# Attention scores as three float32r products, with engine queues ordered by a list schedule

## The chip, the cores and the metric

The kernel runs on one NeuronCore of a Trainium2 chip. The metric is the device time of one execution in microseconds (us); the time before is 1512.19 us, the median of 3 runs (1509.23 to 1512.96). Engines are named as in the profile: PE is the matrix engine (its weight loads, PEld, overlap its matmuls), DVE the vector engine, ACT the scalar engine, POOL the GpSimd engine; SP issues the DMAs. [...] Each engine takes its instructions in the order in which they stand in its queue, and waits at an instruction whose inputs are not ready.

## The reference

One transformer block in fp32: attention with 16 heads of 128 on 2 batches of 1024 tokens and a model width of 512, then a gated feed-forward layer with ternary weights and 1365 hidden columns, each between layer norms and with a residual.

```python
q = jnp.einsum('bsd,hed->bhse', x, W_Q)
k = jnp.einsum('bsd,hed->bhse', x, W_K)
v = jnp.einsum('bsd,hed->bhse', x, W_V)
scores = jnp.einsum('bhse,bhme->bhsm', q, k) * scale
scores = jnp.where(causal, jnp.float32(-1000000000.0), scores)
pattern = jax.nn.softmax(scores, axis=-1)
z = jnp.einsum('bhsm,bhme->bhse', pattern, v)
out = jnp.einsum('bhse,hde->bsd', z, W_O)
...
x = x + _layernorm(_L0_attn_ref(_layernorm(x), W_Q, W_K, W_V, W_O))
x = x + _layernorm(_L0_ffn_ref(_layernorm(x), w1, w3, w2))
```

## The kernel before

Two number formats matter. float32r is a format of PE for 4-byte values that keeps fewer bits of the mantissa. Where the kernel needs an fp32 result from it, it splits an operand into forms: a leading part ("a"), a low part ("l") and a last one ("d", a difference of the two), each exact in float32r. Two products are summed in one PSUM tile `main`, the third goes into a second tile `diff`, and `main` x 4097 - `diff` is the fp32 product (`combine`, lines 453 to 460). Projections of Q, K and V (lines 471, 478, 499) and the output projection (519) are computed so. The scores (line 556) and the products of the softmax weights with V (line 650) are plain fp32 matmuls.

The work goes over 32 heads (n = 0 to 31, 16 for each batch). A head has eight score rows `i` of 128 queries; row i has L = (i + 1) x 128 columns, because of the causal mask. `scores` makes one row: one or two matmuls of at most 512 columns into `s_ps` (two buffers of two PSUM banks each), the mask on the last 128 columns (DVE, line 561), the negated maximum (DVE, 565), the exponential with its sum (ACT, 572), the reciprocal (DVE, 577) and the scaling (ACT, 578) in the SBUF tile `p_sb`, of which there is one for even rows and one for odd. `turn` transposes the row in blocks of 32 into `blocks` (DVE, 604); for each pair of rows a DMA carries them to DRAM (`hop`) and `bring` fetches them back in another order (`pt`, four DMAs), and `values` multiplies them with V and splits the result into forms for the output projection (ACT 662, DVE 667, POOL 670). One pair of heads shares the weights of V and of the output; weights are loaded and split in `load_raw`, `lead_and_low` (ACT 439, POOL 440) and `difference_form` (DVE 446).

The order of the queues is written out by hand. The main loop goes over the score rows of all heads; in each step it does some projections, value products and output products for PE (`fill`, `product`), the scores three rows ahead (`AHEAD`), the transpose of the row two ahead, and one-off work (`side`: weight statistics, ternary weights, the layer norms of the middle, the transposes of the second batch). `behind` and `past` hold an instruction back until a named earlier one stands in its queue, by `tc.issue_after`. The feed-forward stage (from about 1270 us on) runs four blocks of 512 tokens, each with 11 tiles of hidden columns (lines 318 and 933).

## Time and profile before

| | |
|---|---|
| Median of 3 runs | 1512.19 us |
| Span of the profiled execution | 1509.5 us |
| Granted PE clock, mean | 0.997 of full speed |
| Busy of the span: PE, DVE, ACT, POOL | 98%, 72%, 53%, 27% |
| Score matmuls, L556 | 768 records, 289.7 us |
| Mask, L561, and maximum, L565 | 256 each, 75.4 and 193.7 us |
| Exponential, L572, and scaling, L578 | 256 each, 190.0 and 197.7 us |
| Transpose in blocks of 32, L604 | 256, 197.1 us |
| DMA to DRAM and back for the largest pair of rows | 1024 KB in 4.5 us, four of 256 KB in 6.2 us (median, issue to landing) |

The profile is one execution, taken by the hardware profiler. A group line gives the source line, the engine, the operation, the tiles (written <- read), the shape and the count, then after the bar the busy time in us and the mean duration of one in ns, and then the idle time of the engine before it with what ended it. An fp32 matmul of the program is recorded as two MATMUL records. [...] A line of waits reads: who waited, for whom, us in total, how often, and the longest. A line of the timeline begins with the start and the length in us. In a table of stretches, the columns are the length, and for each engine the busy us.

### The profile page before, as it was taken

How to read it: one execution, taken by the hardware profiler on the slowest of the kernel's cores; microseconds unless marked ns; L12 is line 12 of the kernel's file. 1: busy time of each engine (PE TensorE's matmuls, PEld its weight loads, DVE VectorE, ACT ScalarE, POOL GpSimd, SP SyncE). 2: the span in 40 equal slices, each digit the busy share in tenths (PEclk: the TensorE clock that was granted, in tenths of full speed). 3: DMA queues.
4: the chain of work that ended last, by engine and by line, in shares of the span. 5: the costliest groups of instructions: out<-in, count | busy, mean ns of one | idle time of the engine just before them, and what ended most of it. 6: DMA issues, size and time to landing. Idle time of an engine off the chain costs nothing.

```text
span 1509.5 us, 21335 instructions
## 1 busy us (share of the span) xinstructions
PE 1475.6 (98%) x7061; PEld 1184.9 (78%) x7061; DVE 1080.6 (72%) x2123; ACT 792.7 (53%) x1566; POOL 404.3 (27%) x472
## 2 busy tenths in 40 slices
PE   8999999999999999999999999999999999999997
PEld 6778888887878787777778787878787877888885
DVE  7767686878786878787777777777777776664444
ACT  4656555555555555666664555555555464444332
POOL 3222222222223333434433333333322110210010
PEclk9999999999999999999999999999999999999999
DMA  3666767676666675758866666666665677530200
GB/s 123 194 194 186 195 184 200 185 202 184 201 191 172 181 206 183 205 166 249 238 200 190 195 192 196 195 195 189 179 179 166 181 216 228 176 102 19 91 28 29
DMA packets 179894, 263.57 MB, mean 175 GB/s; under 512 B 19188, under 2 KB 120564, under 8 KB 175688
## 3 DMA queue, kind: packets, MB, share of 16 engines
q1 hardware_dynamic: 179784, 262.20, 59.5%
q8 instruction: 57, 0.93, 0.3%
q14 instruction: 53, 0.43, 0.1%
HBM read 160.43 MB, written 101.71 MB: 174 GB/s over the span
## 4 chain that ended last, share of the span: by engine, by line
PE 66%; issue 10%; DVE 9%; DMA 7%; ACT 5%; POOL 2%; SPq 1%; DVEq 0%; POOLq 0%; ACTq 0%
PE mm L650 11%; PE mm L471 10%; PE mm L318 10%; PE s_ps L556 10%; PE mm L499 8%; PE mm L519 6%; PE yp L933 5%; PE mm L478 5%; DVE nm L565 3%; DMA hop<-blocks 2%; ACT p_sb L572 2%; DMA wqk<-wk 2%; ACT p_sb L578 1%; POOL kl L440 1%; DVE blocks L604 1%
## 5 line engine op out<-in xcount | busy, mean ns | idle before, releaser
L572 ACT ACTIVATE p_sb<-s_ps,nm 128x128 f32<-128x128 f32 (+7 forms) x256 | 190.0, 742 | 367.3 <-DVE nm L565 360.8
L556 PE MATMUL s_ps<-k,q 128*128 128x512 f32 (+3 forms) x768 | 289.7, 486 | 0.7 <-ACT p_sb L572 0.7
L650 PE MATMUL mm<-pt,v_sb 128*128 128x256 f32 (+1 forms) x1280 | 271.7, 359 | 11.3 <-ACT q L454 3.7
L650 PEld LDWEIGHTS mm<-pt,v_sb 128*128 128x128 f32 x1280 | 238.1, 190 | 48.8 <-ACT q L454 6.2
L578 ACT ACTIVATE p_sb<-p_sb,ri 128x128 f32<-128x128 f32 (+7 forms) x256 | 197.7, 773 | 33.0 <-DVE ri L577 30.5
L565 DVE TENSOR_REDUCE nm<-s_ps 128x1 f32<-128x128 f32 (+7 forms) x256 | 193.7, 757 | 7.1
L604 DVE STREAM_TRANSPOSE blocks<-p_sb 128x128 f32<-128x128 f32 (+7 forms) x256 | 197.1, 770 | 1.2 <-ACT p_sb L578 0.9
L556 PEld LDWEIGHTS s_ps<-k,q 128*128 128x128 f32 x768 | 132.3, 190 | 69.4 <-issue 61.4
L670 POOL TENSOR_TENSOR zd<-za,zl 128x256 fp32r<-128x256 f32 x128 | 94.7, 739 | 328.0 <-DVE zl L667 319.7
L561 DVE TENSOR_TENSOR s_ps<-s_ps,causal 128x128 f32<-128x128 f32 x256 | 75.4, 295 | 136.1 <-PE s_ps L556 135.6
L499 PE MATMUL mm<-va,xb 128*128 128x256 f32 x512 | 158.5, 310 | 0.0
L499 PE MATMUL mm<-vd,xb 128*128 128x256 f32 x512 | 144.9, 283 | 0.9 <-POOL xb L409 0.9
L499 PE MATMUL mm<-vl,xb 128*128 128x256 f32 x512 | 144.6, 282 | 0.0
L471 PE MATMUL mm<-xb,qa 128*128 128x512 f32 x256 | 119.6, 467 | 1.0 <-ACT xb L407 1.0
L471 PE MATMUL mm<-xb,ka 128*128 128x512 f32 x256 | 112.3, 439 | 0.0
L499 PEld LDWEIGHTS mm<-vl,xb 128*128 128x128 f32 x512 | 97.7, 191 | 7.1 <-issue 4.1
L499 PEld LDWEIGHTS mm<-va,xb 128*128 128x128 f32 x512 | 97.7, 191 | 7.1 <-issue 3.9
L471 PE MATMUL mm<-xb,ql 128*128 128x512 f32 x256 | 101.7, 397 | 0.0
L471 PE MATMUL mm<-xb,kl 128*128 128x512 f32 x256 | 100.7, 393 | 0.1
L499 PEld LDWEIGHTS mm<-vd,xb 128*128 128x128 f32 x512 | 97.7, 191 | 1.1 <-POOL xb L409 1.1
L601 POOL MEMSET blocks<- 128x128 f32 x128 | 26.2, 205 | 263.1 <-DMA hop<-blocks 185.2
L533 DVE TENSOR_TENSOR acc<-acc,mm 128x512 f32<-128x512 f32 x128 | 86.1, 683 | 12.7 <-ACT acc L528 5.4
(162 smaller groups left out, 2777.3 us busy)
## 6 DMA issues: line engine op xcount, KB each, us to landing
hop<-blocks SPq DMA_DIRECT2D x32, 1024.0 KB, 4.5
pt<-hop SPq DMA_DIRECT2D x128, 256.0 KB, 6.2
hop<-blocks SPq DMA_DIRECT2D x32, 768.0 KB, 3.3
pt<-hop SPq DMA_DIRECT2D x128, 192.0 KB, 3.8
hop<-blocks SPq DMA_DIRECT2D x32, 512.0 KB, 3.2
pt<-hop SPq DMA_DIRECT2D x128, 128.0 KB, 3.2
wqk<-wq SPq DMA_DIRECT2D x32, 256.0 KB, 5.2
wqk<-wk SPq DMA_DIRECT2D x32, 256.0 KB, 6.6
```

The lines of the kernel that those rows point to most:

```text
L318: newest[0] = nc.tensor.matmul(ps[:fl, :], lhsT=t[:, c, :], rhs=bl[k][:, c, :], start=(c == 0 and k == 0), stop=(c == NC - 1 and k == 1),)
L471: newest[0] = nc.tensor.matmul(main, lhsT=forms[f][0][:, c, :], rhs=forms[f][1][:, c, :], start=(c == 0 and f == 0), stop=(c == NC - 1 and ...
L499: newest[0] = nc.tensor.matmul((main, main, diff)[f][:, ts(t, 2 * P)], lhsT=forms[f][0][:, c, token], rhs=forms[f][1][:, c, :], start=(t = ...
L519: newest[0] = nc.tensor.matmul((main, main, diff)[f], lhsT=zs[g, t // QT, j][f][:, ts(t % QT, P)], rhs=weights[3, g][f][:, 2 * j : 2 * j + ...
L533: nc.vector.tensor_tensor(dst, dst, diff, ALU.subtract)
L556: newest[0] = nc.tensor.matmul(s_ps[:, ds(k0, kl)], lhsT=proj[n, 0, i // QT][:, ts(i % QT, P)], rhs=proj[n, 1, k0 // TB][:, :kl], start=Tr ...
L565: top = nc.vector.tensor_reduce(nm, s_ps[:, :L], axis=AX.X, op=ALU.max, negate=True)
L572: e = nc.scalar.activation(p_sb[:, :L], s_ps[:, :L], AF.Exp, bias=nm, accum_out=rs)
L578: nc.scalar.mul(p_sb[:, :L], p_sb[:, :L], ri)
L604: turned = nc.vector.transpose(b[:, :, 0 : i + 1, il, :].rearrange("p to t r -> p t to r"), p_sb[:, :L].rearrange("p (b r) -> p b r", r=32),)
L650: newest[0] = nc.tensor.matmul(dst, lhsT=proj[g, 2][:, kt, ts(j, P)], rhs=rhs, start=(kt == 0), stop=(kt == 2 * m + 1),)
L670: nc.gpsimd.tensor_tensor(diff, lead, low, ALU.subtract)
```

## The change

- Q and K are kept in three float32r forms (tiles `q0a`, `q0l`, `q0d` and so on) instead of one fp32 tile. After `combine`, ACT makes the leading form; for Q, DVE makes the low and POOL the last one, for K, POOL the low and DVE the last.
- Each score matmul becomes three float32r matmuls, two into `sm` and one into `sd` (one PSUM bank and two buffers each, in place of the two buffers of `s_ps`). ACT copies `sm`, scaled by -4097, into `p_sb`; DVE applies the mask there (signs are turned, so a maximum), and one DVE instruction per piece of 512 columns adds `sd` and takes the minimum. The exponential reads `p_sb`.
- `issue_after` and the holds of `behind`, `past` and `busy` are gone. All pools are made through `Order`, which knows the tiles, and at the end `arrange` finds the dependences, gives each instruction a cost, runs a list schedule forwards and backwards ten times, keeps the shortest, and fixes each engine's order (SP's DMAs too) by it.
- The transposes of the first batch use `sm` and `sd` buffers; the DMA scratch of the program is set to 512 bytes.

```diff
@@ query_key_unit
-            proj[n, kind, k] = qkpool.tile(
-                [P, TB], FP, name=f"{'qk'[kind]}{k}", bufs=2 if kind == 1 and k == 0 else 1
+            bufs = 2 if kind == 1 and k == 0 else 1
+            raw, lead, low, last = (
+                qkpool.tile([P, TB], dt, name=f"{'qk'[kind]}{k}{f}", bufs=bufs)
+                for f, dt in (("d", FP), ("a", FR), ("l", FR), ("d", FR))
             )
...
-                combine(
-                    proj[n, kind, k], main, diff, SCALE if kind == 0 else 1.0
-                )
+                combine(raw, main, diff, SCALE if kind == 0 else 1.0)
+                if kind == 0:
+                    nc.scalar.mul(lead, raw, LEAD / T12)
+                    nc.vector.scalar_tensor_tensor(
+                        low, lead, -T12, raw, ALU.mult, ALU.add
+                    )
+                    nc.gpsimd.tensor_tensor(last, lead, low, ALU.subtract)
+                else:
+                    nc.scalar.mul(lead, raw, LEAD)
+                    nc.gpsimd.tensor_tensor(low, raw, lead, ALU.subtract)
+                    nc.vector.scalar_tensor_tensor(
+                        last, low, -T12, lead, ALU.mult, ALU.add
+                    )
+                proj[n, kind, k] = lead, low, last
@@ behind (past and busy likewise)
-            with ExitStack() as order:
-                for name in names:
-                    k = len(marks[name]) - 1
-                    k = k if of is None else min(of, k)
-                    order.enter_context(tc.issue_after(marks[name][k]))
-                yield
+            yield
@@ scores
-            s_ps = ps_s.tile([P, S], FP, name="s_ps")
-            for k0 in range(0, L, TB):
-                kl = min(TB, L - k0)
-                newest[0] = nc.tensor.matmul(
-                    s_ps[:, ds(k0, kl)], lhsT=proj[n, 0, i // QT][:, ts(i % QT, P)],
-                    rhs=proj[n, 1, k0 // TB][:, :kl],
-                    start=True, stop=True,
-                )
-            nc.vector.tensor_tensor(
-                s_ps[:, ts(i, P)], s_ps[:, ts(i, P)], causal, ALU.min
-            )
-            nm = small.tile([P, 1], FP, name="nm")
-            top = nc.vector.tensor_reduce(
-                nm, s_ps[:, :L], axis=AX.X, op=ALU.max, negate=True
-            )
+            q = [w[:, ts(i % QT, P)] for w in proj[n, 0, i // QT]]
+            chunks = [(k0, min(TB, L - k0)) for k0 in range(0, L, TB)]
+            diffs = []
+            for k0, kl in chunks:
+                main = ps_s.tile([P, TB], FP, name="sm")[:, :kl]
+                diff = ps_s.tile([P, TB], FP, name="sd")[:, :kl]
+                diffs.append(diff)
+                for f, dst in enumerate((main, main, diff)):
+                    newest[0] = nc.tensor.matmul(
+                        dst, lhsT=q[f], rhs=proj[n, 1, k0 // TB][f][:, :kl],
+                        start=f != 1, stop=f > 0,
+                    )
+                nc.scalar.mul(p_sb[:, ds(k0, kl)], main, -(T12 + 1.0))
+            nm = KEPT
+            for (k0, kl), diff in zip(chunks, diffs):
+                if k0 + kl == L:
+                    nc.vector.tensor_tensor(
+                        p_sb[:, ts(i, P)], p_sb[:, ts(i, P)], causal, ALU.max
+                    )
+                least = small.tile([P, 1], FP, name="nm", bufs=6)
+                top = nc.vector.tensor_tensor_reduce(
+                    p_sb[:, ds(k0, kl)], p_sb[:, ds(k0, kl)], diff, 1.0, nm,
+                    ALU.add, ALU.min, accum_out=least,
+                )
+                nm = least
             rs = small.tile([P, 1], FP, name="rs")
             e = nc.scalar.activation(
-                p_sb[:, :L], s_ps[:, :L], AF.Exp, bias=nm, accum_out=rs
+                p_sb[:, :L], p_sb[:, :L], AF.Exp, bias=nm, scale=-1.0, accum_out=rs
             )
@@ class Order, arrange, at its end
+        order = self.lists(ops, engine, preds)
+        for chain in order.values():
+            for j, k in zip(chain, chain[1:]):
+                self.tc.add_manual_dep(
+                    ops[k], ops[j].name,
+                    mybir.DependencyInfo(
+                        mybir.DependencyClass.NoSync, mybir.DependencyReason.DATA
+                    ),
+                    reason="order",
+                )
@@ class Order, lists
+        rank, best = list(range(n)), None
+        for _ in range(PASSES):
+            start, took, order = work.forward(rank)
+            end = max(map(sum, zip(start, took)))
+            if best is None or end < best[0]:
+                best = end, start, took, order
+            rank = work.backward(start, took)
@@ class Work, forward
+        for _ in range(n):
+            t, e, k = self.next(wait, here, free)
+            order[e].append(k)
+            busy, took = self.costs[k]
+            if self.table[k] not in (0, table):
+                table, busy, took = self.table[k], busy + 1290, took + 1290
+            if e == "SP":
+                wire = max(wire, t) + self.size[k] / 260
+                took = max(1900 + self.size[k] / 260, wire - t + 1500)
+            start[k], tooks[k], free[e] = t, took, t + busy
+            for j in self.follows[k]:
+                ready[j] = max(ready[j], t + self.lag(k, j, took))
+                missing[j] -= 1
+                if not missing[j]:
+                    ripe(j)
@@ the end of the kernel
+    pools.arrange()
@@ kernel
-    nc = bacc.Bacc("TRN2", target_bir_lowering=False, num_devices=1)
+    nc = bacc.Bacc(
+        "TRN2", target_bir_lowering=False, num_devices=1, dynamic_dma_scratch_size=512
+    )
```

`forward` takes, on each engine, the ready instruction of the lowest rank; `backward` computes from the end how late each instruction may start, and that is the next rank.

## The prediction

> **What bounds the kernel now.** I read the page's shares first, then PE's own waits, then the starts of single matmuls in the timeline.

> ```profile
> PE 1475.6 (98%) x7061; PEld 1184.9 (78%) x7061; DVE 1080.6 (72%) x2123; ACT 792.7 (53%) x1566; POOL 404.3 (27%) x472
> ...
> PE mm L650 <- ACT q L454: 3.7, 6, 0.9
> PE mm L650 <- DVE acc L530: 3.2, 2, 1.7
> ...
> 704.31 0.39 PE L471 MATMUL mm<-xb,kl 128*128 128x512 f32 x1
> 704.54 0.39 PE L471 MATMUL mm<-xb,ka 128*128 128x512 f32 x1
> ...
> 179.78 0.28 PE L499 MATMUL mm<-vl,xb 128*128 128x256 f32 x1
> 179.90 0.28 PE L499 MATMUL mm<-vd,xb 128*128 128x256 f32 x1
> ...
> 702.17 0.19 PEld L556 LDWEIGHTS s_ps<-k,q 128*128 128x128 f32 x1 [0.24 <-issue]
> 702.60 0.19 PEld L556 LDWEIGHTS s_ps<-k,q 128*128 128x128 f32 x1 [0.24 <-issue]
> ```

> PE is hardly ever named as waiting (a few us in total). Its busy share overstates, because matmul records overlap; the price of a matmul is the distance to the next start. A float32r matmul of 512 columns costs 0.227 us, one of 256 columns 0.120. An fp32 matmul is recorded as two passes of 0.430 each at 512 columns (0.323 at 384, 0.216 at 256, 0.109 at 128: median starts on L556 and L650), so four times as much per column. Counts times price: 3,360 float32r matmuls of 512 columns (L471, L478, L519, L318, L933) 762.7; 1,536 of 256 (L499) 184.3; value products on L650, 1,024 x 0.216 + 256 x 0.109 = 249.1; scores on L556, per head 4 x 0.109 + 4 x 0.216 + 4 x 0.323 + 12 x 0.430 = 7.75, times 32 = 248.1; 111 transposes 12.1. Sum 1456. The span of 1509.5 is this, plus 1.5 before the first matmul, 9.9 after the last, and 41.7 of waits and slow clock, 12 of them in the first 50 us. So PE's instruction stream sets the time, and about 30 us of waits lie in its middle.

> The other engines, over the ten stretches of 100 us from 150 to 1150 (sum and mean), and the start of the same output products one pair of heads apart in the chain:

> ```profile
> sum 1000.00, PE 987.86 PEld 791.64 DVE 759.16 ACT 550.11 POOL 309.08; mean PE 98.79 PEld 79.16 DVE 75.92 ACT 55.01 POOL 30.91
> ...
> 107.32 4.12 PE mm L519 x18
> 183.21 4.12 PE mm L519 x18
> ```

> A head takes 75.9 / 2 = 37.9 us, of which DVE is busy 28.8, ACT 20.8, POOL 11.7.

> **The change, part by part.** *Scores.* Each fp32 matmul becomes three float32r ones: per head 18 of 512 columns (4.09), 6 of 384 (0.174 on the line through the two measured points: 1.04), 6 of 256 (0.72) and 6 of 128. No row shows float32r at 128 columns: the line gives 0.066, the transposes with 128 columns show 0.109, two fp32 passes 0.218. I take 0.109, the row with this size and a 4-byte operand: 0.65. Sum 6.50 a head, 208.1 in all, a saving of 39.9 us (48 with 0.066, 19 with 0.218). [...] Nothing covers this term: it is PE time.

> *New work on ACT, per head.* 12 copies of the main product out of PSUM, 4,608 columns: rows of 590 ns at 512 and 378 at 256 give 166 + 0.83 a column, 5.8 us; four leading forms at 0.62 (L439), 2.5; exp from SBUF, +0.03 x 8. 20.8 + 8.5 = 29.3.

> *DVE.* The 8 maxima go (6.05 by L565's 193.7 / 32). 12 fused add-and-minimum instructions come, each with a second instruction that reads the accumulator. Nearest for the first is the maximum by form, 290 at 128 and 689 at 512: 157 + 1.04 a column; for the second the one-column L577, 150. 12 x 0.307 + 4.8 = 8.5, net +2.4 (+0.6 without the second instruction; +7.2 if the fused one makes two passes). Four low and last forms at 0.684 (L458): +2.7. The mask of 128 columns moves from PSUM to SBUF at the same 0.295. Together +5.1: 33.9.

> ```profile
> L565 DVE TENSOR_REDUCE nm<-s_ps 128x1 f32<-128x512 f32 x32 | 22.0, 689 | 0.6
> L565 DVE TENSOR_REDUCE nm<-s_ps 128x1 f32<-128x128 f32 x32 | 9.3, 290 | 1.1
> L458 DVE SCALAR_TENSOR_TENSOR q<-mm,q 128x512 f32<-128x512 f32 x64 | 43.8, 684 | 7.8 <-ACT q L454 6.6 <-PE mm L478 1.2
> ...
> 15.29 3.42 POOL L440 TENSOR_TENSOR vl<-wvo,va 128x512 fp32r<-128x512 f32 x2
> 15.80 1.77 DVE L446 SCALAR_TENSOR_TENSOR qd<-ql,qa 128x512 fp32r<-128x512 f32 x1
> ```

> *POOL* gets four subtractions a head at 1.29 (L440): 11.7 + 5.2 = 16.9. The last two rows show what that may cost: a DVE instruction with two SBUF inputs took 1.77 instead of 0.67 while POOL ran. [...] Over the whole run L446 lost little (738 on average against a median of 674), so I add 0.5 a head for the new ones (8 masks, 4 forms); if each lost 1.1 us it would be 13.

> A head then needs PE 37.9 - 1.25 = 36.7, DVE 34.4, ACT 29.3, POOL 16.9: PE stays the longest.

> *The added wait.* The score row now sits in its p_sb tile from the first copy to the DVE transpose, and there is one tile for even rows, one for odd. So the copy of row i+2 waits on ACT for the transpose of row i; behind it on ACT stand the exp of row i+1 and the evacuations that free PSUM for PE. Rows of 1,024, 768, 512 and 256 columns need, end to end (copies, mask, fused pass, exp 0.19 over its scaling row, reciprocal 0.15, scaling by L578, transpose by L604), 7.0 + 5.9 + 4.2 + 3.0 = 20.1 us plus some 28 hand-overs of 0.1. That is 22.9 of 36.7, so each row may queue 3.4 us for free.

> *The queues.* The hand-written order (issue_after) goes; a list schedule fixes each engine's order. On PE it places the first value product a median of 20 to 23 us of PE work behind the score rows that it needs, against 20 to 24 before, so the DMA round trip keeps its cover. SP issues the same 1,010 DMAs, at new places; POOL's new forms stand in one queue with the clearing of blocks, which waited 185 us for DMAs before, and a form stuck there would hold up the next head's scores. Of the 30 us of waits, about 12 are eight single waits of 1 to 2 us beside one-off work (588 to 755 and 1251 us). A schedule that counts that work may save half of them (6); it may also lose as much: -6, bounds -12 and +12.

> Sum on the profiled execution: 1509.5 - 39.9 - 6 = 1463.6. The median of the runs shown is 2.7 above it: 1466.

> **The rivals.**
> *The schedule closes the middle too* (all of those waits, and float32r at 0.066): 1512 - 48 - 25 = 1439, as far as 1452. For it: single matmuls now fill gaps. Against: ACT and DVE are fuller, and the startup and the tail remain.
> *The p_sb pair becomes tight.* DVE at 94% of a head means that a row queues at each of its three DVE steps. At 0.2 us over the free 3.4, four rows and 32 heads add 26: 1492; with 0.3, 1504. Against: in the present trace the long waits of a row are only those before the transpose, which is put off by the hand-written order.
> *The slower one: DVE takes over.* It decides from 9.1 us of added DVE work a head (28.8 + 9.1 = 37.9). A two-pass fused instruction (+7.2) and the forms (+2.7) make 38.7, so 0.8 x 32 = 26 us slower: 1538. For it: no row shows the fused instruction, and POOL contention grows. Against: the rows by form put it at 5.1 to 5.6.
> *The change doesn't do what it says:* float32r at 128 columns for two fp32 passes leaves 19 of the 39.9: 1487. It is in the range.

> **How the numbers follow.** Forecast 1466, 55%, its own range 1453 to 1480. Closing the middle 14%. The p_sb pair, with the dear 128 columns, 17%, one in ten of it ending near no change. DVE 14%, of which 3 is no change and 11 slower. This kernel's measurement tells 0.3%, 4.5 us, from nothing. Faster 0.55 + 0.14 + 0.15 = 0.84; same 0.05; slower 0.11. The range runs from 1443, into the second case, to 1502, through most of the third.

> **What would show it.** Right: float32r score matmuls 0.227 apart at 512 columns, PE named for few waits, the same output products some 73.4 apart per pair of heads, DVE near 90 per 100 us. Wrong: a fused instruction over 0.9 us at 512 columns; ACT's copies waiting for the transpose and PE for that copy; POOL forms waiting behind the clearing; 128-column starts over 0.11.

## The result, and the profile after

The changed kernel takes 1527.67 us (median of 4 runs, 1524.69 to 1533.79) beside 1512.38 us for the kernel before: a ratio of 1.011, 95% interval [1.0087, 1.0132]. The forecast was 1466 us, range 1443 to 1502: wrong in sign.

The engines' row and the chain's shares, from the page of the changed kernel:

```profile
PE 1464.0 (96%) x7445; PEld 1242.0 (81%) x7445; DVE 1267.1 (83%) x2763; ACT 1011.9 (66%) x2078; POOL 590.5 (39%) x600
...
PE 64%; DVE 20%; issue 6%; ACT 4%; DMA 4%; SPq 1%; POOL 1%; DVEq 0%; POOLq 0%; ACTq 0%
```

The chain's shares before:

```profile
PE 66%; issue 10%; DVE 9%; DMA 7%; ACT 5%; POOL 2%; SPq 1%; DVEq 0%; POOLq 0%; ACTq 0%
```

DVE's share of the chain that ended last went from 9% to 20%. PE's named waits add up to 51.5 us; before, they add up to 23.7 (the prediction says "a few us in total"). The longest of them after (who waited, for whom, us in total, times, longest):

```profile
PE sd L875 <- DVE nm L887: 13.0, 19, 2.1
PE sd L875 <- DVE k0d L799: 7.6, 11, 2.0
PE mm L837 <- DVE acc L848: 4.7, 4, 1.6
PE tr L708 <- DVE acc L427: 4.5, 2, 4.1
```

All four are waits for DVE. In the first, the third score product finds both `sd` banks still held by fused passes that DVE has not reached; in the second, the key's last form is late.

The same sum as in the prediction (count times distance between starts) splits the span. The float32r score matmuls are priced at 0.227 apart at 512 columns, 0.176 at 384, 0.120 at 256 and 0.112 at 128. Their medians in this run, with the starts that waited among them, are 0.229, 0.180, 0.120 and 0.1145, which would be 2.4 us more in all; 0.112 is the median of e15, told below, where PE waits least. Rows of the timeline after (start, length):

```profile
870.01 0.40 PE L875 MATMUL sm<-k0a,q1a 128*128 128x512 f32 x1
870.25 0.40 PE L875 MATMUL sm<-k0l,q1l 128*128 128x512 f32 x1
870.48 0.39 PE L875 MATMUL sd<-k0d,q1d 128*128 128x512 f32 x1
870.71 0.22 PE L875 MATMUL sm<-k1a,q1a 128*128 128x128 f32 x1
870.77 0.27 PE L875 MATMUL sm<-k1l,q1l 128*128 128x128 f32 x1
871.68 0.33 PE L875 MATMUL sd<-k1d,q1d 128*128 128x128 f32 x1 [0.64 <-DVE nm L887]
...
312.25 0.22 PE L875 MATMUL sm<-k1a,q1a 128*128 128x128 f32 x1
312.31 0.27 PE L875 MATMUL sm<-k1l,q1l 128*128 128x128 f32 x1
312.42 0.28 PE L875 MATMUL sd<-k1d,q1d 128*128 128x128 f32 x1
312.53 0.65 PE L972 MATMUL mm<-pt,v_sb 128*128 128x256 f32 x2
```

At 312.25 nothing is waited for: behind the first 128-column product the next one starts after 0.06, behind the second and the third after 0.11. Only 43 of the 192 starts lie under 0.065.

At these prices, PE's stream is 1417.5 us, 39.0 less than the 1456.5 before. The rest of the span, with 1.4 us before the first matmul and 9.5 after the last taken off, is time in which PE waits or runs at a slow clock: 97.6 us, where it was 41.7. So -39.0 + 55.9 - 0.5 (the two ends) = +16.4, which but for rounding is the difference of the two spans (1526.0 and 1509.5). The expectations of the experiments take 0.058 for every 128-column product, and so speak of 50 us gained on the stream, 67 us of added waits, and 66 us of waits in e3. Where that time lies (us of it in each stretch; two of the experiments told below stand beside it):

| stretch of the span | before | after | after, DVE cost corrected in the list (e11) | the same, mask in PSUM (e15) |
|---|---|---|---|---|
| 0 to 100 | 14.0 | 24.0 | 15.4 | 20.5 |
| 100 to 400 | 2.1 | 10.0 | 8.4 | 4.2 |
| 400 to 800, with the one-off work | 14.0 | 41.0 | 23.6 | 12.6 |
| 800 to 1200 | 6.3 | 13.5 | 12.0 | 3.4 |
| 1200 to the end | 5.4 | 9.1 | 5.0 | 3.7 |
| all | 41.7 | 97.6 | 64.4 | 44.4 |

DVE is not full even so. Over the ten stretches of 100 us from 150 to 1150, after:

```profile
sum 1000.00, PE 966.73 PEld 829.41 DVE 895.81 ACT 721.26 POOL 457.84; mean PE 96.67 PEld 82.94 DVE 89.58 ACT 72.13 POOL 45.78
```

What DVE's time went into, by form, after:

The mask and the `qd` form before:

```profile
L561 DVE TENSOR_TENSOR s_ps<-s_ps,causal 128x128 f32<-128x128 f32 x256 | 75.4, 295 | 136.1 <-PE s_ps L556 135.6
...
L446 DVE SCALAR_TENSOR_TENSOR qd<-ql,qa 128x512 fp32r<-128x512 f32 x32 | 22.4, 699 | 1.9 <-POOL ql L440 1.9
```

The fused pass is as forecast (0.675 at 512 columns, its accumulator read 0.082). The instructions with two SBUF inputs are not: the mask takes 0.410 where it took 0.295 on PSUM, and the `qd` form, which the change does not touch, 1.241 where it took 0.699. They are longer beside POOL, which works on SBUF alone in this kernel: the mask took 0.28 on average in the 124 cases without a POOL instruction (other than a clearing) beside it, and 0.53 in the 132 with one; the last forms of all weights (L751) took 0.67 in 69 cases without and 1.21 in 59 with. The fused pass at 512 columns, which has one input in SBUF, took 0.68 and 0.69, and the mask on PSUM before took 0.30 and 0.29. The summed DVE durations grew by 240.7 us (7.5 a head); its busy time, which counts once where the records of neighbours overlap, grew by 186.5 (5.8 a head). What single instructions took beyond the median of their shape grew from 26 to 129 us, 3.2 a head.

How that reaches PE shows in one place of the timeline after (start, length; rows of DVE, then POOL, then PE):

```profile
402.04 1.76 DVE L518 SCALAR_TENSOR_TENSOR raw<-raw,scales,tmp 128x512 f32<-128x512 f32 x1
403.73 1.35 DVE L883 TENSOR_TENSOR p_sb<-p_sb,causal 128x128 f32<-128x128 f32 x1
405.22 0.75 DVE L887 CUSTOM_DVE_ANT_0 p_sb<-p_sb,sd,nm 128x512 f32<-128x512 f32 x1
...
405.89 1.11 DVE L926 STREAM_TRANSPOSE blocks<-p_sb 128x896 f32<-128x896 f32 x1
406.92 0.65 DVE L799 SCALAR_TENSOR_TENSOR k0d<-k0l,k0a 128x512 fp32r<-128x512 f32 x1
...
401.97 1.28 POOL L795 TENSOR_TENSOR q0d<-q0a,q0l 128x512 fp32r<-128x512 f32 x1
403.21 1.71 POOL L798 TENSOR_TENSOR k0l<-k0d,k0a 128x512 fp32r<-128x512 f32 x1
...
404.98 0.33 PE L875 MATMUL sm<-k0l,q0l 128*128 128x128 f32 x1 [0.70 <-POOL k0l L798]
405.14 0.44 PE L778 MATMUL mm<-xb,ka 128*128 128x512 f32 x1
407.63 0.47 PE L875 MATMUL sd<-k0d,q0d 128*128 128x128 f32 x1 [2.04 <-DVE k0d L799]
```

While POOL makes `q0d` and `k0l`, DVE's weight sum takes 1.76 us (0.75 at its median) and the mask 1.35 (0.29). `k0l` itself is late, 1.71 where POOL's subtractions have a median of about 1.3. `k0d`, 0.65 us of work, has its input from 404.92 on and starts at 406.92, behind the fused pass and the transpose in DVE's queue, and PE, whose own order is fixed too, stands 2.04 us before the product that reads it.

### The profile page after: what moved, and what is told of

Read it like the earlier page. It is cut to its first block, busy times and chain, and to the rows that moved or that the text cites. A ratio compares the mean times of both kernels' runs of the same rounds, so it can differ in the third digit from the quotient of the medians.

```text
span 1526.0 us, 24028 instructions
## 1 busy us (share of the span) xinstructions
PE 1464.0 (96%) x7445; PEld 1242.0 (81%) x7445; DVE 1267.1 (83%) x2763; ACT 1011.9 (66%) x2078; POOL 590.5 (39%) x600
## 4 chain that ended last, share of the span: by engine, by line
PE 64%; DVE 20%; issue 6%; ACT 4%; DMA 4%; SPq 1%; POOL 1%; DVEq 0%; POOLq 0%; ACTq 0%
PE mm L972 12%; PE mm L778 11%; PE mm L622 9%; PE mm L817 7%; PE mm L837 7%; PE sm L875 5%; PE mm L785 5%; PE yp L1250 5%; PE sd L875 3%; DVE p_sb L887 3%; DVE p_sb L883 2%; DVE blocks L926 2%; DMA hop<-blocks 2%; DVE acc L848 1%; DVE acc L851 1%
## 5 line engine op out<-in xcount | busy, mean ns | idle before, releaser
L894 ACT ACTIVATE p_sb<-p_sb,nm 128x128 f32<-128x128 f32 (+7 forms) x256 | 198.8, 776 | 192.2 <-DVE nm L887 191.3
L972 PE MATMUL mm<-pt,v_sb 128*128 128x256 f32 (+1 forms) x1280 | 281.6, 365 | 6.0 <-DMA pt<-hop 3.0
L992 POOL TENSOR_TENSOR zd<-za,zl 128x256 fp32r<-128x256 f32 x128 | 106.8, 834 | 251.2 <-DVE zl L989 232.7
L879 ACT ACTIVATE p_sb<-sm 128x512 f32<-128x512 f32 (+3 forms) x384 | 176.3, 484 | 25.3 <-PE sm L875 19.1
L887 DVE CUSTOM_DVE_ANT_0 p_sb<-p_sb,sd 128x512 f32<-128x512 f32 (+3 forms) x256 | 148.0, 579 | 19.4 <-ACT p_sb L879 1.8
L817 PE MATMUL mm<-va,xb 128*128 128x256 f32 x512 | 144.7, 283 | 0.0
L883 DVE TENSOR_TENSOR p_sb<-p_sb,causal 128x128 f32<-128x128 f32 x256 | 105.0, 410 | 3.5 <-ACT p_sb L879 3.3
L778 PE MATMUL mm<-xb,qa 128*128 128x512 f32 x256 | 102.3, 400 | 1.0 <-ACT xb L712 1.0
L633 DVE SCALAR_TENSOR_TENSOR sg<-mm,scales,sg 128x512 f32<-128x512 f32 (+1 forms) x41 | 30.5, 744 | 80.6 <-PE mm L622 79.7
L837 PE MATMUL mm<-od,zd 128*128 128x512 f32 x256 | 83.8, 398 | 4.1 <-DVE k1d L761 2.0
```

The costliest lines, as they stand in the source:

```text
L778: newest[0] = nc.tensor.matmul(main, lhsT=forms[f][0][:, c, :], rhs=forms[f][1][:, c, :], start=(c == 0 and f == 0), stop=(c == NC - 1 and ...
L817: newest[0] = nc.tensor.matmul((main, main, diff)[f][:, ts(t, 2 * P)], lhsT=forms[f][0][:, c, token], rhs=forms[f][1][:, c, :], start=(t = ...
L837: newest[0] = nc.tensor.matmul((main, main, diff)[f], lhsT=zs[g, t // QT, j][f][:, ts(t % QT, P)], rhs=weights[3, g][f][:, 2 * j : 2 * j + ...
L879: nc.scalar.mul(p_sb[:, ds(k0, kl)], main, -(T12 + 1.0))
L883: nc.vector.tensor_tensor(p_sb[:, ts(i, P)], p_sb[:, ts(i, P)], causal, ALU.max)
L887: top = nc.vector.tensor_tensor_reduce(p_sb[:, ds(k0, kl)], p_sb[:, ds(k0, kl)], diff, 1.0, nm, ALU.add, ALU.min, accum_out=least,)
```

## The experiments

Three theories stood at first. D: POOL holds DVE's instructions off, and DVE, nearly full, passes that to PE. S: the list's order itself is at fault. P: the score row's chain in its `p_sb` tile is too long. Times below are medians beside 1511.8 to 1513.2 us for the kernel before on the same chip; the ratio is to that.

**e1, the order alone.** Scores, forms and PSUM buffers as before, under `Order` and `arrange`.

```diff
-                main = ps_s.tile([P, TB], FP, name="sm")[:, :kl]
-                diff = ps_s.tile([P, TB], FP, name="sd")[:, :kl]
...
+            s_ps = ps_s.tile([P, S], FP, name="s_ps")
...
+                    s_ps[:, ds(k0, kl)], lhsT=proj[n, 0, i // QT][:, ts(i % QT, P)],
+                    rhs=proj[n, 1, k0 // TB][:, :kl],
```

> The list schedule alone, with the scores as before (fp32 matmuls, mask and maximum in PSUM). Theory D (DVE is too full, because of the added forms and because its instructions with two SBUF inputs are held off while POOL runs): DVE is as light as before, so the order loses nothing; 1490 to 1512 us, PE's waits at most the 41.7 us of before, DVE near 76 per 100 us. Theory S (the order that the list makes is at fault): slower than before by much of the lost 67 us of waits, 1540 or more.

Measured 1501.41, ratio 0.9918 [0.9902, 0.9935]. The list by itself gains 12 us. Its ten stretches:

```profile
sum 1000.00, PE 996.14 PEld 799.05 DVE 769.18 ACT 549.00 POOL 313.08; mean PE 99.61 PEld 79.91 DVE 76.92 ACT 54.90 POOL 31.31
```

PE's waits in the whole span are 33 us (1500.8 less the stream's 1456.5 and 11.0 at the two ends). That list schedules as such lose time is out.

**e2, the scores alone.** The new scores and forms in the hand-written order (lines against the changed kernel).

```diff
+                    order.enter_context(tc.issue_after(marks[name][k]))
...
-    pools.arrange()
```

> The three float32r products and the fused pass alone, under the hand-written order of before. Theory D: DVE stays at 88 or more per 100 us and PE waits as much or more; 1520 to 1580 us. Theory S: the gain of 50 us on PE's stream arrives, 1460 to 1480. If the pair of p_sb tiles were the cause (theory P), it would show here too, with ACT's copy of sm waiting for the transpose, since the hand order puts the transpose off.

Measured 1665.69, ratio 1.1003 [1.0987, 1.102]: 153 us slower, with DVE busy for only 78 of 100 us in the ten stretches. D's and S's numbers are missed by far, and ACT's copies wait for the transpose for 5.5 us in all, so P's sign is missing too. Waits of DVE and of PE in this run:

```profile
DVE p_sb L588 <- ACT p_sb L580: 45.9, 30, 5.3
...
DVE p_sb L584 <- ACT p_sb L580: 40.4, 54, 2.3
```

```profile
PE sd L576 <- DVE nm L588: 30.4, 64, 1.1
```

The exponential's wait for the row's last DVE step is not new (327 us here, 361 before). New are DVE's waits for ACT's copies (3.3 and 1.8 us in the changed kernel's rows of the mask and the fused pass) and most of PE's for the `sd` bank. The reading, argued and not tested alone, is that an order made for the short chain of the fp32 scores does not fit the long one, with a copy and a pass for each piece. So the scores and the order interact: the list is worth 12 us under the old scores and 138 under the new (1665.7 to 1527.7).

**e3, the mask back on PSUM.** It is applied to `sd`, which the fused pass adds.

```diff
-                        p_sb[:, ts(i, P)], p_sb[:, ts(i, P)], causal, ALU.max
+                        diff[:, kl - P :], diff[:, kl - P :], causal, ALU.max
```

> The changed kernel with the mask applied to sd in PSUM and not to p_sb in SBUF: 256 DVE instructions with two SBUF inputs become such with one. Theory D: the mask falls from 410 ns to about 295, DVE loses 30 us of busy time, and the time falls by 10 to 30 us, to 1498 to 1518. Theories S and P: within 5 us of 1527.

Measured 1486.76, ratio 0.9829 [0.9814, 0.9844]: 41 us less than the changed kernel for one operand, more than D expected. The waits of PE in this run:

```profile
PE mm L972 <- DMA pt<-hop: 8.1, 6, 3.3
...
PE sd L875 <- DVE k0d L799: 1.5, 3, 0.7
PE sd L875 <- DVE nm L887: 1.4, 4, 0.6
```

The waits for `nm` (13.0) and `k0d` (7.6) are all but gone. The mask no longer has two SBUF inputs (0.289 for 0.410), and no longer waits for ACT's copy.

**e4, POOL's new subtractions left out.** Another form stands in for each form that they made, so the scores are other numbers.

```diff
-                    nc.gpsimd.tensor_tensor(last, lead, low, ALU.subtract)
...
-                    nc.gpsimd.tensor_tensor(low, raw, lead, ALU.subtract)
```

> The changed kernel without the subtractions on POOL that make the last form of Q and the low form of K (128 instructions of 1.3 to 1.5 us; another form stands in their place, so the scores are other numbers, with the same matmuls). Theory D: DVE's instructions with two SBUF inputs come back to near their undisturbed times, DVE falls by 40 to 80 us and the time to 1465 to 1505. Theory S: 1515 or more. Theory P: within 10 us of 1527, since a row holds its p_sb tile as long as before.

Measured 1491.96, ratio 0.9854 [0.9839, 0.9869]. It gains 36 us (29 against the mean of the three plain orders, e6 and e10 below being the other two), though POOL is off the path. DVE is busy for 1214 us instead of 1267, which fits POOL's work costing time through DVE; but the key's last form has no step on POOL to wait for here either, so this run alone doesn't tell the two apart.

**e5, the mask in PSUM with other DVE work in its place.** z's low part made twice, which gives 128 more two-input instructions outside the score row.

```diff
+                nc.vector.scalar_tensor_tensor(
+                    low, lead, -T12, copy, ALU.mult, ALU.add
+                )
```

> e3 (mask on sd in PSUM, 1486.8 us) with the low form of z made twice: 128 more DVE instructions of 256 columns with two SBUF inputs, as many columns as the 256 masks of 128 that e3 relieved, but outside the chain of a score row. Theory D (DVE too full, two-SBUF-input instructions held off by POOL): the gain of e3 goes again, 1510 to 1535 us. Theory P (e3 gained because a row holds its p_sb tile for a shorter time): within 8 us of 1487.

Measured 1503.36, ratio 0.9943 [0.9928, 0.9958]. DVE is busy for 1268 us, as in the changed kernel, and 17 of the 41 us are given back, between what the theories expected. Beside the mean of the two orders with the mask in PSUM (e3 and e12 below, 1492) it is 11, so the load's part in the gain is not shown.

**e6, another order of the same quality.** Plain DVE costs in the list raised by 4 ns, matmul latency by 5 ns.

```diff
-            return 72 + 1.042 * n, 158 + 1.042 * n
+            return 76 + 1.042 * n, 162 + 1.042 * n
...
-            return t, t + 165
+            return t, t + 170
```

> The changed kernel with the list schedule's cost of a plain DVE instruction raised by 4 ns and of a matmul's latency by 5 ns: the same work, in an order that differs by chance. It measures how far the order alone scatters. If the gains of e3 and e4 are real, within 8 us of 1527; if they were luck of the order (theory S), off by 20 or more.

Measured 1513.35, ratio 1.0006 [0.9997, 1.0015]: 14 us away for a change that means nothing, between the two expectations. With e10 and e12 below, orders of one kernel lie up to 14 us apart, so no single difference under 15 is read as a cause.

**e7, the list told of the hold-off.** DVE instructions with two SBUF inputs cost 0.5 ns a column and 50 ns more in the list; the work is the same.

```diff
-            return 72 + 1.042 * n, 158 + 1.042 * n
+            both = [
+                a for a in i.ins
+                if getattr(a, "bass_ap", None) is not None and not self.in_psum(a)
+                and math.prod(k for _, k in a.ap[1:]) > 1
+            ]
+            held = 0.5 * n + 50 if len(both) > 1 else 0
+            return 72 + 1.042 * n + held, 158 + 1.042 * n + held
```

> The changed kernel with the same work, but the list schedule is told that a DVE instruction with two SBUF inputs takes longer (0.5 ns a column and 50 ns more). Theory S in its milder form (the plan is made with wrong durations, and the order breaks where they differ): 1490 to 1510 us. Theory D (the work itself is too much for DVE): 1515 to 1530, since no order takes work off DVE.

Measured 1494.82, ratio 0.9888 [0.9873, 0.9903]: 33 us less than the changed kernel, with the same instructions. DVE is fuller (92.1 per 100 us) and the mask takes longer still (0.464, row below), so D in its plain form, that a DVE this full must stop PE, falls.

```profile
L889 DVE TENSOR_TENSOR p_sb<-p_sb,causal 128x128 f32<-128x128 f32 x256 | 118.9, 464 | 3.5 <-ACT p_sb L885 3.3
```

**e8, a longer row.** One more instruction on ACT between the reciprocal and the scaling.

```diff
+            ri2 = small.tile([P, 1], FP, name="ri2")
+            nc.scalar.copy(ri2, ri)
-            nc.scalar.mul(p_sb[:, :L], p_sb[:, :L], ri)
+            nc.scalar.mul(p_sb[:, :L], p_sb[:, :L], ri2)
```

> The changed kernel with an extra one-column ACT copy of the reciprocal between the reciprocal and the scaling: each row holds its p_sb tile some 0.3 to 0.4 us longer, DVE does nothing more, ACT 256 x 0.2 us. Theory P: four rows of one parity and 32 heads, 0.35 x 4 x 32 = 45, so 1550 to 1580 us. Theory D: 1525 to 1537.

Measured 1541.52, ratio 1.0186 [1.0168, 1.0204]: 14 us more than the changed kernel, within what a new order alone may do. That is below what P expected, and a step from one order to another may do as much, so it says little.

**Second round.** e7 left two readings: the list has to know where DVE is held off, or only how much DVE has to do. The formulas of `cost` for DVE, summed over the changed kernel's instructions, give 1099 us of planned occupancy; the page has DVE busy for 1267. So the plan believes in 168 us of DVE time that isn't there, and e7's added costs come to about 160. (For the kernel before the gap is 96 us: 985 planned, 1081 busy.)

**e9, e7's costs with the mask in PSUM**, the edits of both.

> The mask on sd in PSUM (1486.8 alone) together with list costs that add 0.5 ns a column and 50 ns to DVE instructions with two SBUF inputs (1494.8 alone). D (the order breaks because POOL holds such instructions off and the plan doesn't know it): the remaining held instructions, the forms and z's low part, are planned right too, PE idle falls from 66 us to 45-60, time 1465-1481. S (each order falls somewhere in a scatter of some 15 us, and 1487 was a lucky draw): 1480-1505, either side of 1487.

Measured 1474.79, ratio 0.9754 [0.9733, 0.9774], inside D's interval and below S's. Whether it is the placing of the costs, as D has it, is what e11 and e15 ask.

**e10, a second order of the same quality** (-4 and -5 ns, the edit of e6 with the other sign).

> The changed kernel with the list costs of plain DVE instructions lowered by 4 ns and the matmul latency by 5 ns: another order that knows nothing more. S: anywhere from 1495 to 1530. D: 1508-1532, as the two such orders so far (1527.7 and 1513.4), and not as low as the 1494.8 of the order with held-off costs.

Measured 1521.66, ratio 1.006 [1.0043, 1.0076], inside both intervals.

**e11, the same sum spread over all DVE instructions.**

```diff
-                return 145 + 1.042 * n, 290 + 1.042 * n
+                return 213 + 1.042 * n, 358 + 1.042 * n
...
-                return 80 + 0.78 * n, 160 + 0.78 * n
+                return 148 + 0.78 * n, 228 + 0.78 * n
-            return 72 + 1.042 * n, 158 + 1.042 * n
+            return 140 + 1.042 * n, 226 + 1.042 * n
```

> The changed kernel with 68 ns added in the list to the cost of every DVE instruction, about the same sum (some 160 us) as the costs that gave 1494.8, but spread without regard to which instructions are held off. If the gain comes from knowing where the hold-off falls (D), this stays at 1508-1532. If a plan that only takes DVE for fuller does it, 1490-1502. S: anywhere from 1495 to 1530.

Measured 1494.47, ratio 0.9886 [0.9871, 0.99]: as e7. What the list needed was the sum; where the hold-off falls made no difference. Its engines and the first of its PE waits:

```profile
PE 1448.1 (97%) x7445; PEld 1239.5 (83%) x7445; DVE 1275.5 (85%) x2763; ACT 1014.9 (68%) x2078; POOL 590.9 (40%) x600
```

```profile
PE sd L875 <- DVE nm L887: 11.8, 12, 2.0
PE mm L972 <- DMA pt<-hop: 6.3, 8, 1.4
...
PE sd L875 <- DVE k0d L799: 1.7, 3, 1.0
```

Planned 1099 + 162 = 1261, busy 1275.5: now they agree. The waits for the key's form are gone; those for the `sd` bank stay, and it takes the mask's move to end them (0.6 us in e15).

**e12, another order of e3** (the edit of e6).

> The mask on sd in PSUM with the list costs of plain DVE instructions raised by 4 ns and the matmul latency by 5 ns. D: the gain of the mask belongs to the work, so within 10 of 1486.8. S: 1480-1515; over 1505 the 41 us of the mask would be mostly luck of the order.

Measured 1497.37, ratio 0.9905 [0.989, 0.9919]. That is just outside D's interval and inside S's. Some 10 of e3's 41 us were luck of the order; the two orders with the mask in PSUM average 1492, the three without 1521.

**Third round.** L: a plan with too little DVE load breaks, but only where DVE is nearly full. Against it stand slack of any kind, and H: that the hold-off costs time even in a plan with the right sum.

**e13, e1 with its DVE sum corrected** (planned 985, busy 1095; 50 ns added).

> The list schedule with the fp32 scores as before (1501.4 with the plain costs), with 50 ns added in the list to every DVE instruction, which closes the gap between its planned DVE load and the measured one (985 planned, 1095 busy). L (a plan whose DVE load is too small breaks only where DVE is nearly full): DVE has room here, so 1494-1506. Slack in general (any plan that takes DVE for fuller gets better): 1475-1492.

Measured 1500.94, ratio 0.9933 [0.9915, 0.9951], as e1. Where DVE has room, its planned sum doesn't matter. Its ten stretches:

```profile
sum 1000.00, PE 998.13 PEld 802.41 DVE 757.54 ACT 558.32 POOL 311.07; mean PE 99.81 PEld 80.24 DVE 75.75 ACT 55.83 POOL 31.11
```

**e14, e4 with its DVE sum corrected** (48 ns).

> POOL's subtractions for Q and K left out, as in the run that gave 1492.0, with 48 ns added in the list to every DVE instruction, which closes its gap (1099 planned, 1214 busy). L (only the sum of the plan counts): 1482-1496, near the 1494.5 of the changed kernel with its gap closed. H (the hold-off costs time even where the plan has the right sum): 1462-1480.

Measured 1482.96, ratio 0.981 [0.9789, 0.9831]. At the edge of L's interval, 12 us below e11, which is within the scatter. What the new forms' hold-off costs beyond the plan is 12 us or less, and isn't told from nothing.

**e15, e3 with its DVE sum corrected** (50 ns).

> The mask on sd in PSUM (1486.8 and 1497.4 in two orders with plain costs), with 50 ns added in the list to every DVE instruction (1099 planned, 1219 busy). L: the same as with the added costs placed on the held-off instructions, 1468-1482. If it counts there where the cost is placed: 1483-1497.

Measured 1474.70, ratio 0.9754 [0.974, 0.9769], as e9. Its engines, its chain and its ten stretches:

```profile
PE 1439.3 (98%) x7445; PEld 1237.7 (84%) x7445; DVE 1208.8 (82%) x2763; ACT 1019.3 (69%) x2078; POOL 584.5 (40%) x600
...
PE 79%; DVE 7%; DMA 5%; ACT 3%; issue 2%; POOL 2%; SPq 1%; DVEq 0%; POOLq 0%; ACTq 0%
```

```profile
sum 1000.00, PE 991.55 PEld 864.62 DVE 889.49 ACT 761.84 POOL 475.24; mean PE 99.16 PEld 86.46 DVE 88.95 ACT 76.18 POOL 47.52
```

DVE is as full as in the changed kernel (88.95 and 89.58 per 100 us), PE at 99.16 against 96.67. The same output products stand 73.2 us apart per pair of heads (860.7, 933.9, 1007.1), where the prediction said 73.4 and the kernel before has 76.5 there.

**e16, half as much again** (102 ns in place of 68).

> The changed kernel with 102 ns added in the list to every DVE instruction, half as much again as closes its gap (68 ns gave 1494.5). L: the right sum is the best, so 1492-1510. Slack in general: 1478-1491.

Measured 1517.87, ratio 1.0035 [1.0021, 1.0049]. Both expectations are missed: L's by 8 us, slack's by 27. More slack isn't better: this is 23 us above e11, and among the orders with the list's own costs. PE now waits longest for the rows that come back by DMA (6.3 us in e11):

```profile
PE mm L972 <- DMA pt<-hop: 13.6, 13, 2.6
```

The four orders with the right sum reproduce one another whatever the placing (1494.8 and 1494.5; 1474.8 and 1474.7). The five with the list's own costs scatter (1513 to 1528; 1487 and 1497). One thing these edits leave together: each raises in the plan both the time for which an instruction holds DVE and the time until its result is there. Which of the two the plan lacked was not tested.

## Why the prediction was wrong

*The scores* were right: 39.0 us saved, 39.9 forecast. The dear 128 columns weighed 0.109 and took 0.112 to 0.115 in the median; the straight line's 0.066 would have been wrong.

*The fused pass* was right: 7.8 a head with its accumulator reads, 8.5 forecast. POOL's new forms waited for DVE (59.2 us for `q1l`); the clearing of blocks waited less for DMAs than before (114.6 us, 185.2 before).

*The contention* was mis-sized. The twelve new instructions took 52.7 us, 1.6 a head, beyond the median of their shape (masks 31.5, the two forms 12.4 and 8.8), where the step put 0.5. The rest of the 3.2 is in instructions that were there before, such as the weights' `qd` and z's low form, for which it put nothing. The step took the mean loss on L446, in a kernel whose POOL is busy for 31 of 100 us, for a kernel with 46. That DVE's busy time nevertheless grew by 5.8 a head, with 5.6 forecast (5.1 and 0.5), is luck: the step added durations to busy time, and the overlap of the records took back what the contention put on.

*The queues* are the step that failed. "A schedule that counts that work may save half of them (6); it may also lose as much: -6, bounds -12 and +12." Under the old scores the list did save 12. Under the new ones PE's waits grew by 56 us. The step judged the list as a method and never looked at the costs that it plans with: its table gives DVE 1099 us where the page has it busy for 1267. For the kernel before, the same formulas give 985 where the page said 1081, and that could be worked out before any run. With the sum corrected, and nothing else, 33 us come back (26 against the mean of three plain orders).

*"PE stays the longest"* holds: 89.6 of 100 us is not full. What does not follow is that PE then doesn't wait. The engines' orders are fixed at build time, so a DVE with 10% to spare and a plan 13% short (168 of 1267) is late at the place where PE next needs it. Rows that share two `sd` banks cannot run ahead (13.0 us of PE's waits for `nm`).

*The rivals.* "DVE takes over" had the sign, not the mechanism: it wanted 9.1 us of added DVE work a head, the busy time grew by 5.8 (186.5 / 32), and e7 and e11 run with a DVE above 92. The `p_sb` pair shows no sign of being tight: ACT's copies waited 5.0 us in all for the transpose. Its hand-overs, put at 0.1 us, took 0.03 to 0.09 in the median in the trace before.

*The signs.* DVE came near 90 per 100 us and the 512-column products stood 0.229 apart in the median, where 0.227 was forecast. PE was not named for few waits, and the same output products stood 74.3 to 77.2 apart per pair of heads (between 824.9 and 1127.6), not 73.4. Of the signs of being wrong only the 128-column starts over 0.11 came true, and they cost nothing against the sum. None of the signs asked whether the list's plan would hold.

*The account of the spans.* Forecast 1463.6, measured 1526.0: +62.4. The scores make +0.9 of it, the edges -0.5, the waits +61.9 (97.6 for the forecast's 35.7). Of the 97.6, 33 go with the corrected sum (e11) and 20 more with the mask in PSUM (e15), while 44 stay, against 33 for the list under the old scores (e1). How much of these 20 is the shorter hold of the `sd` bank and how much the lighter DVE was not separated; e5 was meant to tell and stayed within the scatter. What makes up the last 9 or so above the forecast stays open.

The version of e15 (or e9) beats both kernels, at 1474.7 us, 9 above the forecast. The changed kernel's own work under a corrected plan (e11, 1494.5) is inside the forecast's range too. So PE's work was priced about right, and the order was not.

## What to carry to other kernels

Where a scheduler fixes the order of in-order queues, hold its cost table against the profile first: sum the planned time of each engine over its instructions and compare with the busy time on the page. Here the gap cost time where DVE was busy for 90% of a stretch, and nothing at 76% (e13). Try a mask or another small two-input step on the operand that is already in PSUM where POOL works on SBUF beside it (here worth about 20 us, 1494.5 to 1474.7); and plan the same kernel two or three times with meaningless changes before reading a difference of 1% as a cause.

## What the runs showed of the hardware

Some waits cost PE more than their length. With the 2.04 us wait shown above, the granted clock (third column from the end) fell, though PE had been busy for a third of the stretch:

```profile
404.00:408.00 4.00, 1.26 (x7) 0.81 (x6) 3.86 (x7) 1.83 (x4) 2.62 (x3) 0.92 0.86 220
408.00:412.00 4.00, 4.00 (x14) 3.21 (x14) 2.58 (x6) 2.64 (x7) 0.00 (x0) 0.66 1.09 325
```

From 407.32 to 410.73, 3.4 us, the trace has it at 0.50, and in that stretch 512-column products, 0.227 apart in the median of the run, start 0.43 apart:

```profile
408.43 0.63 PE L778 MATMUL mm<-xb,ka 128*128 128x512 f32 x1
408.86 0.63 PE L778 MATMUL mm<-xb,kl 128*128 128x512 f32 x1
```

The changed kernel's trace has five such stretches of 3.4 us at 0.50, beside waits of PE of 1.94, 2.04, 2.15 and 2.72 us and one of 1.11 with two shorter ones behind it, and one of 10.2 us at the start; single waits of 1.16 to 1.56 us elsewhere in it have none. The kernel before has one of 3.4 us, at the start, and both have one after the last matmul. The mean clock is 0.989, before 0.997: by an estimate at most some 12 of the 56 us (0.008 x 1526).

POOL's instructions are longer beside DVE's too. z's last form on POOL (L992) takes 0.834 us on average, and took 0.739 before: 0.74 in the 45 cases without one of DVE's instructions with two SBUF inputs (masks, forms, weight sums) beside it, 0.88 in the 83 with one.
